# Three deformable convolutions and an expert network on one core: border rows skipped, side work paced by the tap

## The chip, the cores and the metric

The kernel runs on one core of a Trainium2 chip. The core has five engines, each with its own queue of instructions: TensorE (PE) multiplies matrices and transposes tiles, VectorE (DVE) does arithmetic on tiles in on-chip memory, ScalarE (ACT) copies, scales and evaluates functions, GpSimd (POOL) here issues the gathers, and SyncE (SP) issues most of the other transfers. Each engine works through its own instructions in order, so an instruction that waits holds up all that stand behind it on that engine. PE reads on-chip memory (SBUF) and writes accumulators (PSUM), from which ACT or DVE copies.

The metric is the time of one execution in microseconds (us). Three runs of the kernel before took 7496.17 to 7528.83 us, with a median of 7508.25 us.

## What is computed

The input is four images of 256 channels and 64 x 64 positions. Each image is normalised over its channels and goes through three layers of a modulated deformable 3 x 3 convolution. The result is added to the input, each position (token) is normalised, and a network of eight experts, of which the two likeliest are taken for each token, is added:

```python
om = conv3x3(x, w_off) + b_off            # zero padding; 27 channels
off, mask = om[:, :18], sigmoid(om[:, 18:])
ys, xs = grid + tap + off                 # for each of 9 taps
sampled = bilinear(x, ys, xs) * mask      # zero outside the image
x = relu(einsum('bikhw,oik->bohw', sampled, wk) + b)      # three times
t = tokens(image + x)
p, e = top_k(softmax(norm(t) @ gate_w + gate_b), 2)
out = t + sum(p * (gelu(norm(t) @ W1[e] + b1[e]) @ W2[e] + b2[e]))
```

The convolution in the first line is the offset convolution. Its input is padded with zeros, so at the first row of an image the upper row of taps adds nothing, and at the last row the lower one.

## The kernel before

**Blocks and stages.** An image is cut into eight blocks (n = 0 to 7) of eight rows, 512 positions each. One layer of one image is a stage. The twelve stages run in a fixed order, written as (layer, image): (0,0), (1,0), (0,1), (2,0), (1,1), (0,2), (2,1), (1,2), (0,3), (2,2), (1,3), (2,3). They are counted from 0 here. Except between stages 0 and 1, between 10 and 11, and at the end, a stage uses nothing that the stage just before it makes, and the pipeline runs on over its border.

**The main work of a block** is `main_block` (L482). For each of nine taps it takes four samples of 128 positions, in two pairs. For each sample (`samples`, L494), POOL gathers the four corners from a table in device memory (L503, ten buffers g), DVE combines them in two instructions (L509, L514, eight buffers s), and ACT scales the result (L517). Two pairs later (`LAG` = 2), `turn` (L521) lets PE transpose the pair into PSUM (L532, tag tp, three buffers) and ACT copy it to sT (L535). After the second pair, `finish` (L541) multiplies sT by the weights of the tap into the accumulator acc (L555). After the ninth tap ACT applies relu (L577). In layers 0 and 1 the result goes into a window, a tile of ten rows: the block's eight and one neighbouring row on each side.

**Windows and plans.** `window` (L281) takes a window's tile. In block 0 it sets the row above the image to zero with a memset on DVE (L290), in block 7 the row below (L292). `rows_done` (L295) copies the shared rows between neighbouring windows on ACT (L300, L301) and starts, for a finished block n, its `store_table` and the `off_block` of block n - 1 (in block 7 of both 6 and 7). `store_table` (L313) transposes the rows (L325), copies them (L328, tile hv, two buffers) and stores them into the table of the next layer, four transfers a time on SP. `off_block` (L345) makes the plan of a block for the next layer: 18 matmuls of the offset convolution into po (L357), a copy with bias on ACT (L366, tile om), four matmuls that turn it to positions (L371, tile pm, one of the three buffers with tag tp), tanh and a copy on ACT (L387 and L391, tiles th and pos), and then 14 short DVE instructions (L395 to L427) that give the row indices idx and the weights cf. The tiles om, th, pos and those of the 14 instructions have one buffer each.

**Other side work.** `pre_block` (L429) loads a block of an image, transposes it (L442), copies it (ACT L447), normalises it on DVE (L55 to L80, in which L62 takes the statistics and L78 writes the result h), stores it into the first table, transposes it back (L462) and fills a window. The first image is done ahead of all stages; image 1 beside stage 0, image 2 beside stage 3, image 3 beside stage 6. `tokens` (L587) follows each block of layer 2: it loads the image's rows (L596), adds them on DVE (L599), transposes (PE L608, ACT L613), multiplies by the gate (L618), stores t (L626), normalises (L62 to L78), stores z (L636), works out the softmax with an exponential on ACT (L661) and the sum on DVE (L665), and picks two experts. When a group of blocks is complete, its expert work is put into queues of small pieces (`routes`, `tiles`, `sums`), of which `pump` takes some after each tap of the later stages.

**What sets the order.** Each piece of side work is a Python generator whose `yield`s cut it into steps. `aside(steps, gen, plan)` (L997) puts it `steps` times into one of two lists, `plans_side` for `off_block` and `side` for the rest. After each tap k, `step` (L1001) takes from the front of each list the number of entries left, divided by the taps left (9 - k) and rounded up, and runs one step for each. One piece with seven entries alone in its list thus runs one step a tap; with two pieces in a list, two steps are run a tap, and both may belong to the same piece. `after(self.last)` places a DVE instruction of side work behind the newest L514. `settle` (L1012) empties both lists at the two dependent borders and at the end, with `draining` set while expert pieces are used up there; `starting` is set until the first stage begins. A scheduler then fixes each engine's final order from these issues and their dependences.

Of the kernel before, what the change touches and what calls it, by code (L numbers as in the profile page):

```python
# [117 lines left out]
class Weave:  # L118
# [162 lines left out]
    def window(self, n, nm, spare):  # L281

        if spare:
            if n % 2 == 0:
                self.spare = self.wt.tile([P, 2, WINN], F32, tag="wt", name=f"win_{nm}")
            w = self.spare[:, n % 2, :].rearrange("p (c r w) -> p c r w", c=CC, w=W)
        else:
            w = self.win.tile([P, CC, RPB + 2, W], F32, tag="win", name=f"win_{nm}")
        if n == 0:
            self.nc.vector.memset(w[:, :, 0, :], 0.0)  # L290
        if n == NB - 1:
            self.nc.vector.memset(w[:, :, RPB + 1, :], 0.0)  # L292
        return w

    def rows_done(self, l, b, n, wins):  # L295

        nc = self.nc
        w = wins[n]
        if n > 0:
            nc.scalar.copy(w[:, :, 0, :], wins[n - 1][:, :, RPB, :])  # L300
            nc.scalar.copy(wins[n - 1][:, :, RPB + 1, :], w[:, :, 1, :])  # L301
        if l > 0:
            self.aside(3, self.store_table(l, b, n, w))
        ready = [n - 1] * (n > 0) + [n] * (n == NB - 1)
        for m in ready:
            gen = self.off_block(l, b, m, wins[m])
            if self.starting and m >= NB // 2:

                self.later.append(gen)
            else:  # L310
                self.aside(6, gen, True)

    def store_table(self, l, b, n, w):  # L313

# [30 lines left out]
    def off_block(self, l, b, n, w):  # L345
# [4 lines left out]

        po = self.ps1.tile([P, BLK], F32, tag="po", name=f"po_{nm}")

        terms = [(ky, kx, c) for kx in (1, 0, 2) for ky in range(3) for c in range(CC)]
        for m, (ky, kx, c) in enumerate(terms):
            g = m % NQ
            x0, x1 = max(0, 1 - kx), min(W, W + 1 - kx)
            nc.tensor.matmul(  # L357
                po[g * Q : (g + 1) * Q, :].rearrange("q (r w) -> q r w", w=W)[:, :, x0:x1],
                lhsT=self.wo[l][:, 3 * ky + kx, c, :],
                rhs=w[:, c, ky : ky + RPB, x0 + kx - 1 : x1 + kx - 1],  # L360
                start=(m < NQ),
                stop=(m + NQ >= len(terms)),
                tile_position=(0, g * Q),
            )
# [26 lines left out]
        nc.scalar.copy(pos.rearrange("p (t k) d -> p t (k d)", k=K), pm[:, :, : 2 * K])  # L391
        yield
        yield
        with self.after(self.last):
            nc.vector.tensor_tensor(  # L395
                pos, pos, self.base[:, n].rearrange("p t k d -> p (t k) d"), ALU.add
# [32 lines left out]
    def pre_block(self, b, n, wins, spare):  # L429
# [8 lines left out]
        for t0 in range(0, TPB, 2):  # L438
# [7 lines left out]
                    )  # L446
            nc.scalar.copy(h[:, t0 : t0 + 2, :], tp)  # L447
        yield
        rest = normalise(nc, self.small, h, h, EPS_C, nm)
        with self.after(self.last):  # L450
            next(rest)
# [89 lines left out]
    def finish(self):  # L541
# [36 lines left out]
        if l < NL - 1:  # L578
            self.rows_done(l + 1, b, n, wins)
        else:  # L580
            self.aside(7, self.tokens(b, n, r))

# [2 lines left out]
    def tokens(self, b, n, r):  # L587
# [37 lines left out]
        nc.scalar.copy(lg, lp)  # L625
        nc.sync.dma_start(self.t_dram[b][n], tok)  # L626
        yield
        rest = normalise(nc, self.small, tok, z, EPS_T, nm)
        with self.after(self.last):
            mean = next(rest)  # L630
# [29 lines left out]
        )  # L660
        nc.scalar.activation(lg, lg, AF.Exp)  # L661
        yield
        sm = small("sm", (P, TPB))
        with self.after(self.last):
            nc.vector.tensor_reduce(sm, lg, AX.X, ALU.add)  # L665
# [335 lines left out]
    def step(self, k):  # L1001

        for side in (self.plans_side, self.side):
            for _ in range(-(-len(side) // (K - k))):
                next(side.pop(0), None)

    def after(self, newest):

# [26 lines left out]
    def run(self):  # L1035
# [36 lines left out]
        for i, (l, b) in enumerate(self.stages):  # L1072
            wins, pre = {}, {}
            for n in range(NB):
                for gen in self.later[:2]:
                    self.aside(6, gen, True)
                self.later = self.later[2:]
                self.main_block(i, n, wins)
                if i in beside:
                    self.aside(5, self.pre_block(beside[i], n, pre, i == 0))  # L1080
            if i + 1 == len(self.stages) or self.stages[i + 1] == (l + 1, b):
                while self.pairs:
                    self.turn()
# [52 lines left out]
```

## Time and profile before

| | before |
|---|---|
| median of three runs | 7508.25 us (7496.17 to 7528.83) |
| the profiled execution's own time | 7520.62 us |
| its span in the profile | 7518.9 us |
| mean clock granted to TensorE | 0.944 |
| PE busy | 6443.2 us, 86% |
| DVE busy | 4952.9 us, 66% |
| POOL busy | 4476.5 us, 60% |
| ACT busy | 3266.0 us, 43% |
| bytes read and written | 313 GB/s over the span |

The groups of the profile give a line's engine, its tile, count, busy time and mean ns, and behind the bar the idle time of the engine ahead of it and what ended that. These are the groups of the lines that the change touches or that wait near it:

```
L357 PE MATMUL po<-win,wo 128*32 128x504 f32 (+1 forms) x2304 | 366.0, 615 | 6.5 <-ACT win L301 4.2 <-ACT win L577 2.0
L357 PE MATMUL po<-win_pre,wo 128*32 128x504 f32 (+1 forms) x1152 | 184.2, 617 | 2.0 <-ACT om L366 2.0
L395 DVE TENSOR_TENSOR pos<-pos,base 128x72 f32<-128x72 f32 x96 | 22.0, 229 | 92.2 <-ACT pos L391 91.7 <-issue 0.5
L665 DVE TENSOR_REDUCE sm_tok<-lg_tok 128x4 f32<-128x32 f32 x32 | 5.8, 182 | 87.2 <-ACT lg_tok L661 83.2 <-ACT sT L535 4.0
L290 DVE MEMSET win<- 128x128 f32 x8 | 1.3, 165 | 72.9 <-PE po L357 71.6 <-PE tp L532 1.3
L292 DVE MEMSET win<- 128x128 f32 x8 | 1.3, 165 | 0.0
L290 DVE MEMSET win_pre<- 128x128 f32 x4 | 0.7, 165 | 26.2 <-PE po L357 25.3 <-PEq L1126 0.9
L292 DVE MEMSET win_pre<- 128x128 f32 x4 | 0.7, 165 | 10.0 <-PE po L357 10.0
```

po's 18 matmuls go to four column tiles of 32 in turn; the hardware lists each as two records, so 96 blocks give 3456. A tile's name carries the kind of block that made it: win_pre, h_pre and st_pre belong to `pre_block`, t_tok, st_tok, lg_tok and sm_tok to `tokens`. In the timeline, each row gives the start, the length, the engine, the line, the operation and, in brackets, the idle time before it with what ended it. "issue" is a wait for nothing that the profile shows, "remote" and "an unknown queue" one for something that it can't name, such as a transfer.

### The profile page before, as it was taken

To read this page: it belongs to the slowest core of one execution; us is meant where nothing else is said; L and a number is where in the kernel's file an instruction comes from. 1 tells how busy PE (TensorE), PEld (TensorE's weight loads), DVE (VectorE), ACT (ScalarE), POOL (GpSimd) and SP (SyncE) were. 2 spreads that over 40 slices of the span, in tenths; PEclk is the share of its full clock that TensorE was granted. 3 is DMA by queue.
4 is the path that set the end of the run, shared out by engine and by line. 5 is a ranking of instruction groups with operands and counts; after the bars stand their busy time and mean duration, and the time that the engine had idled before them with its cause. 6 is when DMAs were issued, how large, how long until landed. Compare 5 with 4: busy or idle time off the path is not lost.

```text
span 7518.9 us, 88985 instructions
## 1 busy us (share of the span) xinstructions
PE 6443.2 (86%) x26500; PEld 3618.8 (48%) x26500; DVE 4952.9 (66%) x11467; ACT 3266.0 (43%) x7141; POOL 4476.5 (60%) x4245
## 2 busy tenths in 40 slices
PE   6898888888898888889988888888888788977887
PEld 3443333334454444445554445444544555644565
DVE  6776777768887666567777556666768554667421
ACT  3444544445544444445443434444444333444322
POOL 4654666656666565556557656555656565666543
PEclk8999999999999999999999999999999899989998
DMA  8997999989998888888888888888888777888644
GB/s 266 337 325 274 352 342 335 346 331 356 362 349 311 300 305 297 278 315 322 314 293 316 293 280 314 295 302 294 308 306 299 251 271 240 288 302 287 211 139 123
DMA packets 800320, 2223.73 MB, mean 296 GB/s; under 512 B 104729, under 2 KB 302873, under 8 KB 794081
## 3 DMA queue, kind: packets, MB, share of 16 engines
q0 software_dynamic: 551200, 1947.35, 73.3%
q1 hardware_dynamic: 248640, 270.69, 10.9%
q8 instruction: 215, 3.52, 0.2%
q14 instruction: 265, 2.16, 0.1%
HBM read 2160.68 MB, written 196.40 MB: 313 GB/s over the span
## 4 chain that ended last, share of the span: by engine, by line
PE 69%; ACT 10%; issue 7%; another core or an unknown queue 6%; DVE 4%; DMA 2%; POOL 1%; SPq 0%; ACTq 0%; DVEq 0%; POOLq 0%
PE acc L555 34%; PE tp L532 10%; PE ph L856 7%; PE py L874 6%; PE po L357 6%; ACT sT L535 4%; ACT s L517 3%; DVE g L509 2%; DVE s L514 1%; PE pm L371 1%; ACT hT L866 1%; PE ftp L840 1%; ACT win L577 1%; PE tpv L325 1%
## 5 line engine op out<-in xcount | busy, mean ns | idle before, releaser
L503 POOL DMA_INDIRECT g<-tab,idx x3456 | 3685.4, 1066 | 2371.6 <-DVE s L514 1061.8
L555 PE MATMUL acc<-sT,wk 128*128 128x512 f32 x6912 | 3492.1, 620 | 253.4 <-ACT sT L535 147.5
L509 DVE SCALAR_TENSOR_TENSOR g<-g,cf 128x512 f32<-128x512 f32 x3456 | 2559.2, 742 | 269.1 <-DMA g<-tab,idx 245.5
L514 DVE SCALAR_TENSOR_TENSOR s<-g,cf 128x256 f32<-128x256 f32 x3456 | 1662.7, 483 | 1331.3 <-PE tp L532 729.9
L535 ACT COPY sT<-tp 128x512 f32<-128x512 f32 x1728 | 1002.0, 585 | 2312.0 <-PE tp L532 1553.0
L517 ACT ACTIVATE s<-s,cf 128x256 f32<-128x256 f32 x3456 | 1629.5, 508 | 256.7 <-DVE s L514 160.7
L555 PEld LDWEIGHTS acc<-sT,wk 128*128 128x128 f32 x6912 | 1198.9, 198 | 1106.7 <-issue 816.7
L532 PEld LDWEIGHTS tp<-ident,s 128*128 128x128 f32 x6912 | 893.2, 146 | 1666.2 <-issue 898.9
L532 PE MATMUL tp<-ident,s 128*128 128x128 f32 x6912 | 1287.3, 286 | 439.2 <-ACT s L517 253.8
L856 PE MATMUL ph<-fzT,w 128*128 128x256 f32 x2608 | 720.8, 411 | 78.0 <-ACT fzT L844 28.1
L874 PE MATMUL py<-w,hT 128*128 128x256 f32 x2608 | 671.1, 396 | 103.5 <-ACT hT L866 58.0
L856 PEld LDWEIGHTS ph<-fzT,w 128*128 128x128 f32 x2608 | 506.3, 205 | 212.9 <-issue 69.6
L874 PEld LDWEIGHTS py<-w,hT 128*128 128x128 f32 x2608 | 484.5, 196 | 242.0 <-issue 91.9
L866 ACT ACTIVATE hT<-ph,w 128x256 f32<-128x256 f32 x652 | 281.9, 471 | 616.3 <-PE ph L856 378.2
L812 POOL DMA_INDIRECT zt<-z,tok x326 | 333.8, 1024 | 161.5 <-issue 88.0
L800 POOL DMA_INDIRECT w<-in_W,wrow x163 | 178.0, 1092 | 381.2 <-issue 138.8
L357 PE MATMUL po<-win,wo 128*32 128x504 f32 (+1 forms) x2304 | 366.0, 615 | 6.5 <-ACT win L301 4.2
L892 DVE TENSOR_TENSOR y<-py,w 128x512 f32<-128x512 f32 x163 | 111.9, 686 | 341.5 <-PE py L874 285.1
L915 POOL DMA_INDIRECT gy<-ys,slots x256 | 255.6, 998 | 104.5 <-issue 70.0
L930 DVE SCALAR_TENSOR_TENSOR ta<-gy,cw,ta 128x256 f32<-128x256 f32 x256 | 120.6, 480 | 125.6 <-DMA gy<-ys,slots 78.4
L357 PE MATMUL po<-win_pre,wo 128*32 128x504 f32 (+1 forms) x1152 | 184.2, 617 | 2.0 <-ACT om L366 2.0
L366 ACT ACTIVATE om<-po,bo 128x512 f32<-128x512 f32 x96 | 65.9, 687 | 265.3 <-PE po L357 156.3
(154 smaller groups left out, 2961.0 us busy)
## 6 DMA issues: line engine op xcount, KB each, us to landing
tab<-hv SPq DMA_DIRECT2D x512, 128.0 KB
g<-tab,idx POOLq DMA_INDIRECT x3456
ys<-y SPq DMA_DIRECT2D x163, 256.0 KB
tab<-h_pre SPq DMA_DIRECT2D x128, 256.0 KB
wk<-in_conv_w SPq DMA_DIRECT2D x99, 256.0 KB
xc_pre<-in_x SPq DMA_DIRECT2D x32, 512.0 KB
xr_tok<-in_x SPq DMA_DIRECT2D x32, 512.0 KB
t<-t_tok SPq DMA_DIRECT2D x32, 512.0 KB
```

What stands on the lines that cost most here:

```text
L357: nc.tensor.matmul(po[g * Q : (g + 1) * Q, :].rearrange("q (r w) -> q r w", w=W)[:, :, x0:x1], lhsT=self.wo[l][:, 3 * ky + kx, c, :], rhs= ...
L503: self.gathered = nc.gpsimd.indirect_dma_start(out=g.rearrange("p x s f -> p (x s f)"), out_offset=None, in_=self.table(*self.stages[i]), ...
L509: nc.vector.scalar_tensor_tensor(g[:, :, 0, :], g[:, :, 1, :], cf[:, j, 0:1], g[:, :, 0, :], ALU.mult, ALU.add,)
L514: self.last = nc.vector.scalar_tensor_tensor(s, g[:, 1, 0, :], cf[:, j, 1:2], g[:, 0, 0, :], ALU.mult, ALU.add)
L517: nc.scalar.activation(s, s, AF.Copy, scale=cf[:, j, 2:3])
L532: self.turned = nc.tensor.transpose(tp[:, c, u * P : (u + 1) * P], ss[u][:, c * P : (c + 1) * P], self.ident)
L535: nc.scalar.copy(self.sT[:, :, t0 * P : (t0 + 2) * P], tp)
L555: nc.tensor.matmul(acc[:, o, :], lhsT=self.wk[k][:, c, o * P : (o + 1) * P], rhs=sT[:, c, :], start=(k == 0 and c == 0), stop=(k == K - 1 ...
L812: self.nc.gpsimd.indirect_dma_start(out=zt, out_offset=None, in_=grp.zd, in_offset=bass.IndirectOffsetOnAxis(ap=grp.tok[:, j : j + 1], axi ...
L856: nc.tensor.matmul(ph[:, h, :], lhsT=w1[:, o : o + P], rhs=zT[:, c, :], start=(c == 0), stop=(c == CC - 1),)
L866: nc.scalar.activation(ht[:, h, :], ph[:, h, :], AF.Gelu, bias=w1[:, k : k + 1])
L874: nc.tensor.matmul(py[:, u, :], lhsT=hT[h // 2][:, h % 2, u * P : (u + 1) * P], rhs=w2[:, h * C : (h + 1) * C], start=(h == 0), stop=(h == ...
```

## The change

Three things change.

1. `window` no longer zeroes a row. The offset convolution of block 0 leaves the upper image row out of the matmuls with ky = 0, and that of block 7 the lower row of those with ky = 2: six of the 18 matmuls then have seven rows in place of eight, 448 or 441 columns for 512 or 504. In block 0 the order of ky becomes 1, 2, 0, so that the first matmul into each column tile writes all rows.
2. `step` runs at most one step of each generator a tap: it passes over the entries of generators that it has already moved in this tap, and falls back to the front of the list where there is no other.
3. `pause` gives one more `yield`, except while `starting` or `draining`, at four places ahead of a DVE part: in `off_block` before L395, in `pre_block` before the normalisation, in `tokens` before the normalisation and before the sum L665. The counts of steps grow with it: `off_block` from 6 to 7, `tokens` from 7 to 9, `pre_block` from 5 to 6.

```diff
--- before.py
+++ after.py
@@ -286,10 +286,6 @@
             w = self.spare[:, n % 2, :].rearrange("p (c r w) -> p c r w", c=CC, w=W)
         else:
             w = self.win.tile([P, CC, RPB + 2, W], F32, tag="win", name=f"win_{nm}")
-        if n == 0:
-            self.nc.vector.memset(w[:, :, 0, :], 0.0)
-        if n == NB - 1:
-            self.nc.vector.memset(w[:, :, RPB + 1, :], 0.0)
         return w
 
     def rows_done(self, l, b, n, wins):
@@ -308,7 +304,7 @@
 
                 self.later.append(gen)
             else:
-                self.aside(6, gen, True)
+                self.aside(7, gen, True)
 
     def store_table(self, l, b, n, w):
 
@@ -350,14 +346,17 @@
 
         po = self.ps1.tile([P, BLK], F32, tag="po", name=f"po_{nm}")
 
-        terms = [(ky, kx, c) for kx in (1, 0, 2) for ky in range(3) for c in range(CC)]
+        top, low = int(n == 0), int(n == NB - 1)
+        kys = (1, 2, 0) if top else (0, 1, 2)
+        terms = [(ky, kx, c) for kx in (1, 0, 2) for ky in kys for c in range(CC)]
         for m, (ky, kx, c) in enumerate(terms):
             g = m % NQ
             x0, x1 = max(0, 1 - kx), min(W, W + 1 - kx)
+            y0, y1 = top * (ky == 0), RPB - low * (ky == 2)
             nc.tensor.matmul(
-                po[g * Q : (g + 1) * Q, :].rearrange("q (r w) -> q r w", w=W)[:, :, x0:x1],
+                po[g * Q : (g + 1) * Q, :].rearrange("q (r w) -> q r w", w=W)[:, y0:y1, x0:x1],
                 lhsT=self.wo[l][:, 3 * ky + kx, c, :],
-                rhs=w[:, c, ky : ky + RPB, x0 + kx - 1 : x1 + kx - 1],
+                rhs=w[:, c, ky + y0 : ky + y1, x0 + kx - 1 : x1 + kx - 1],
                 start=(m < NQ),
                 stop=(m + NQ >= len(terms)),
                 tile_position=(0, g * Q),
@@ -391,6 +390,8 @@
         nc.scalar.copy(pos.rearrange("p (t k) d -> p t (k d)", k=K), pm[:, :, : 2 * K])
         yield
         yield
+        for _ in self.pause():
+            yield
         with self.after(self.last):
             nc.vector.tensor_tensor(
                 pos, pos, self.base[:, n].rearrange("p t k d -> p (t k) d"), ALU.add
@@ -446,6 +447,8 @@
                     )
             nc.scalar.copy(h[:, t0 : t0 + 2, :], tp)
         yield
+        for _ in self.pause():
+            yield
         rest = normalise(nc, self.small, h, h, EPS_C, nm)
         with self.after(self.last):
             next(rest)
@@ -578,7 +581,7 @@
         if l < NL - 1:
             self.rows_done(l + 1, b, n, wins)
         else:
-            self.aside(7, self.tokens(b, n, r))
+            self.aside(9, self.tokens(b, n, r))
 
 
 
@@ -625,6 +628,8 @@
         nc.scalar.copy(lg, lp)
         nc.sync.dma_start(self.t_dram[b][n], tok)
         yield
+        for _ in self.pause():
+            yield
         rest = normalise(nc, self.small, tok, z, EPS_T, nm)
         with self.after(self.last):
             mean = next(rest)
@@ -660,6 +665,8 @@
         )
         nc.scalar.activation(lg, lg, AF.Exp)
         yield
+        for _ in self.pause():
+            yield
         sm = small("sm", (P, TPB))
         with self.after(self.last):
             nc.vector.tensor_reduce(sm, lg, AX.X, ALU.add)
@@ -1001,8 +1008,15 @@
     def step(self, k):
 
         for side in (self.plans_side, self.side):
+            moved = []
             for _ in range(-(-len(side) // (K - k))):
-                next(side.pop(0), None)
+                i = next((i for i, gen in enumerate(side) if gen not in moved), 0)
+                moved.append(side.pop(i))
+                next(moved[-1], None)
+
+    def pause(self):
+
+        return range(0 if self.starting or self.draining else 1)
 
     def after(self, newest):
 
@@ -1073,11 +1087,11 @@
             wins, pre = {}, {}
             for n in range(NB):
                 for gen in self.later[:2]:
-                    self.aside(6, gen, True)
+                    self.aside(7, gen, True)
                 self.later = self.later[2:]
                 self.main_block(i, n, wins)
                 if i in beside:
-                    self.aside(5, self.pre_block(beside[i], n, pre, i == 0))
+                    self.aside(6, self.pre_block(beside[i], n, pre, i == 0))
             if i + 1 == len(self.stages) or self.stages[i + 1] == (l + 1, b):
                 while self.pairs:
                     self.turn()
```

## The prediction

> **What bounds the kernel now.** The order of reading is: busy times, chain, VectorE's waits, the timeline at the longest of them, then windows over whole blocks, which give the price.
>
> First the page's busy times and the engine shares of the chain that ended last:
>
> ```profile
> PE 6443.2 (86%) x26500; PEld 3618.8 (48%) x26500; DVE 4952.9 (66%) x11467; ACT 3266.0 (43%) x7141; POOL 4476.5 (60%) x4245
> ...
> PE 69%; ACT 10%; issue 7%; another core or an unknown queue 6%; DVE 4%; DMA 2%; POOL 1%; SPq 0%; ACTq 0%; DVEq 0%; POOLq 0%
> ```
>
> TensorE (PE) is the bound, with 7518.9 - 6443.2 = 1076 us idle. An edit can win only part of that idle time, matmul columns, or a lower clock. Next, what VectorE (DVE) waits for, with sum, count and longest in us:
>
> ```profile
> DVE s L514 <- PE tp L532: 729.9, 626, 9.2
> DVE pos L395 <- ACT pos L391: 91.7, 21, 11.0
> DVE sm_tok L665 <- ACT lg_tok L661: 83.2, 13, 9.0
> DVE win L290 <- PE po L357: 71.6, 6, 14.7
> DVE st_pre L62 <- ACT h_pre L447: 52.6, 12, 9.1
> DVE win_pre L290 <- PE po L357: 25.3, 2, 14.7
> ```
>
> The first is the healthy one: DVE has filled all eight s buffers and waits for PE to free one. The others stop DVE behind a side instruction; rows 2, 3 and 5 are what the pauses delay, rows 4 and 6 are the memsets. The timeline at one memset, a row each of DVE, POOL, ACT and PE (start, length; in brackets the idle time before and what ended it):
>
> ```profile
> 1085.53 0.17 DVE L290 MEMSET win<- 128x128 f32 x1 [10.59 <-PE po L357]
> ...
> 1087.05 1.21 POOL L503 DMA_INDIRECT g<-tab,idx  x1 [10.89 <-DVE s L514]
> ...
> 1104.17 0.58 ACT L328 COPY hv<-tpv 128x512 f32<-128x512 f32 x1 [6.45 <-remote]
> ...
> 1105.22 0.69 PE L532 MATMUL tp<-ident,s 128*128 128x128 f32 x2 [6.32 <-ACT s L517]
> ```
>
> The memset needs a free window, freed only when PE has read an old one. DVE stops 10.6 us, POOL cannot gather 10.9 us, then gathers come in a burst. The hv copy waits 6.5 us for its buffer, ScalarE (ACT) stands, and PE starves 6.3 us. Windows over a quiet block and over this one, the last of its stage (us, PE, PEld, DVE, ACT, POOL busy, PE clock, DMA share, GB/s), then the recovery alone:
>
> ```profile
> 995.80:1051.80 56.00, 50.06 (x197) 22.78 (x197) 43.47 (x87) 28.39 (x64) 38.60 (x36) 1.00 0.95 354
> 1051.80:1118.30 66.50, 53.67 (x202) 24.26 (x203) 45.19 (x91) 29.27 (x65) 37.33 (x36) 0.95 0.86 323
> ...
> 1097.00:1105.00 8.00, 1.33 (x4) 0.30 (x2) 5.67 (x13) 1.42 (x3) 4.73 (x6) 0.78 1.04 408
> ```
>
> The block is 10.5 us longer, at clock 0.95, and in the recovery PE works 1.3 of 8 us. Stages 3 and 9 have no such stall, and their last blocks are still about 4 us over their neighbours (all nine wk loads are there). So one bad memset costs about 7 us, 0.66 per us of stall. It varies: stages 4 and 7 have stalls of 12.2 and 14.7 us, yet last blocks no longer than expected. PE idle in excess of its usual 0.105 per us, counted from a stall's start to 25 us behind it, gives over the memsets of row 0 27.4 us in eight events, largest 7.1.
>
> **The change part by part.**
>
> *Memsets.* 24 instructions of 0.165 us go (4 us of DVE, hidden: DVE is 34% idle), and with them 109 us of wait (72.9 + 26.2 + 10.0 in the groups of L290 and L292). Block lengths give four stalls at 7 us (stages 1, 2, 5, 8), one at 5 (stage 6), 2 for the rest: 35 us. The lower end is 15 (half of the excess idle of 27.4: a delay that PE makes good later), the upper 60 (109 us at the rate 7/10.6 = 0.66, less what stages 4 and 7 show). I take 35, the block count, because it contains the clock. Late next is the border plan, below.
>
> *Columns.* 24 border blocks shorten 6 of 18 po matmuls each by 1/8, 288 records. The four column tiles overlap: 28 records in one run took 3.52 us, 0.126 each, while the row's mean of 615 ns counts each in full. That gives 288 x 0.126 / 8 = 4.5 us; in full it would be 288 x 0.615 / 8 = 22. I take 5, as the run is the wall time. At n = 0 the middle ky now comes first, with equal count; runs of po matmuls are 272 for 278 in the built order. Zero.
>
> *Off-block pause.* From the pos copy on ACT to the add on DVE the built order has four taps of 5.9 us for three. Usual blocks wait nothing either way. In four blocks of image 1's preparation, 1.5 taps become 1.75, which ends waits of about 4 us each beside stage 0, at no loss of PE: zero. The plan has up to five taps left until it is used.
>
> *One step a tap per piece.* This moves most at the stage borders, where the plans of blocks 6 (A) and 7 (B) are both made in the next stage's block 0. Before, A ran all its steps, then B; B's add stood two taps behind its pos copy. Now they alternate; but A's tiles th and pos have one buffer, so B's tanh and pos copy stand in ACT's order behind A's last reads, and B's add on DVE follows 0.25 tap later. DVE runs almost two taps ahead of PE and ACT, so it will wait. How long can be read where before had slack: at one such border the last two rows below are DVE's sample and ACT's scale of two samples later in the same tap.
>
> ```profile
> 1183.15 0.48 DVE L514 SCALAR_TENSOR_TENSOR s<-g,cf 128x256 f32<-128x256 f32 x1
> ...
> 1191.27 0.91 ACT L517 ACTIVATE s<-s,cf 128x256 f32<-128x256 f32 x2
> ```
>
> DVE is done at 1183.63, ACT at 1192.18: 8.5 us. The ten such places give 11.2, 7.1, 8.5, 7.0, 1.0, 4.4, 7.3, 8.2, 14.6 and 7.3, together 76.6 us. Queued behind this add on DVE are the next samples, behind these POOL's gathers and ACT's scales: the memset's pattern. Its price there: the seven memset stalls at stage ends, 86.8 us, cost 33, or 0.38 per us; so 29. The lower end is 0: seven border waits of pos before (43 us, such as 6.0 at 1156.55) leave PE no excess idle, and they go. The upper is ten times 7.1 = 71. I take 29, since the memset is the nearest stall in length. In eight places B's 18 po matmuls also stand as one lump behind A's, before a transpose, where part was spread: 8 x 0.8 = 6 us (0 to 16, two gaps of 0.98 us, the time of a short run). pm then holds one of three tp buffers some five taps. The copy that frees a tp buffer ends 0.6 us after its transposes, so two serve the pairs: zero.
>
> The Trainium skill, "Perfetto Trace Analysis", section "Optimization Strategy", speaks against this: the same gap repeated on the engine that should be full can mean too few buffers for the next tile. By it the 0.68 us gap of a tap would come once more in 8 x 5 taps, 27 us, and the sum would be -22 instead of -49. The trace of before, with pm held briefly, shows neither.
>
> *Token pauses.* The fourteen waits of L665 for the exponential (87.2 us) have 27.0 us of excess PE idle behind them. In stages 9 and 11 the distance grows from 1 tap to 2, in stage 3 from 0.75 to 1.25, in stage 6 it stays 1.0. Waits of 50.7 + 4.0 of 87.2 us therefore go: 27.0 x 0.63 = 17 (10 to 27). The add of xr moves a tap nearer its load: it had 14 to 18 us, has 7 to 10, and landings take 3.5 to 9.5. In a bad case DVE waits 3 us; inside the lower end.
>
> *Statistics pauses.* ACT L447 to the statistics grows from 0.75 to 2.75 taps, ACT L613 from 1.5 to 3: thirteen waits with 8.8 us of excess, of which 7 go. PE's own wait for the normalised h (L462 on L78, up to 4.75 us at 1885.26) mostly goes, as PE's transposes now stand half a tap from it for 1.5: about 25 us of stages 3 and 6, of which I take 20, PE having other waits soon after. Together 27 (5 to 34). SP's stores of t, z and tab and POOL's piece queue move by a tap; the tables are read two stages later and the experts run beside later stages, so zero. Were that cover gone, one tap of 5.9 us per group.
>
> *Sum.* Gains 35 + 5 + 17 + 27 = 84, losses 29 + 6 = 35: -49. The profiled execution took 7520.62, so 7471.6; it lies 12.4 us above the median of the runs, 7508.25, against which it is **7459**.
>
> **The rivals.**
> - *More than the sum* (0.15). "issue" and "unknown queue" hold 13% of the chain, 1019 us; bursts of gathers feed them. Six per cent fewer, 61 us, gives about 7398. For: DMA share 1.04 in the recovery. Against: these shares also stand in stages without a memset.
> - *Nothing to measure* (0.25). DVE's lead absorbs most stalls, as in stages 4 and 7, and stage 6's sums don't move: 7471 to 7545. For: 27 us of excess idle for 109 us of wait. Against: the 10.5 us block.
> - *Slower* (0.19). The border wait takes the memset's place, ten times 7.1 plus lumps of 16 = 87, against gains at their low ends, 15 + 5 + 10 + 5 = 35: +52, 7560. With central gains it turns the sign beyond 7.8 us a place, with low gains beyond 3. For: it holds DVE and POOL at the same place of the pipeline. Against: the old border waits cost nothing.
>
> **How the numbers follow.** A measurement of this kernel tells about 0.5%, 37.5 us: faster is below 7470.7, slower above 7545.8. The forecast, 7425 to 7470, has 0.41; with the first rival, faster is 0.56, same 0.25, slower 0.19. The range goes from 7385 (upper gains in part) to 7565.
>
> **What the profile after would show.** No rows L290 and L292; hv's wait for "remote" (32.4) near nothing; pos waiting about 80 to 100 us for ACT in some ten waits of 7 to 15 us at the first blocks of stages; st and sm waits under half; last blocks of stages 1 and 2 near 60 us and first blocks longer. I am wrong if the last blocks stay at 67, if the border waits starve PE by more than 7 us each, or if tp buffers show up before L532.

## The result, and the profile after

The changed kernel is slower: 7569.73 us (median of six runs, 7564.73 to 7584.75) against 7503.91 us for six runs of the kernel before (7487.89 to 7528.83), a ratio of 1.009 with a 95% interval of 1.0072 to 1.0107. Forecast were 7459 us and a gain. The profiled execution has a span of 7563.0 us, 44 us longer than that of before.

One fact is needed before anything else is read. All experiments ran in a second setting, where the kernel before takes about 6805 us instead of 7504. The record names five chips for them, which agree (medians of 6803 to 6808 us); which chip gave the first setting is not on record, nor what its condition was. In the second setting the same changed kernel is not slower (0.9988). So each ratio below is against the kernel before in the same setting, and the text says which.

The page after, first setting, busy times and chain:

```profile
PE 6419.9 (85%) x26500; PEld 3590.7 (47%) x26500; DVE 4959.8 (66%) x11443; ACT 3269.2 (43%) x7141; POOL 4447.2 (59%) x4245
...
PE 69%; ACT 10%; issue 8%; another core or an unknown queue 6%; DVE 3%; DMA 2%; POOL 1%; SPq 0%; ACTq 0%; DVEq 0%; POOLq 0%
```

TensorE is busy 23 us less and idle 67 us more. VectorE's waits after, first setting (sum, count, longest):

```profile
DVE pos L396 <- ACT pos L390: 121.3, 27, 13.0
DVE r L602 <- DMA xr_tok<-in_x: 81.1, 13, 9.6
DVE r L602 <- ACT r L580: 46.8, 8, 10.3
DVE st_pre L62 <- ACT h_pre L448: 26.7, 6, 10.5
DVE sm_tok L672 <- ACT lg_tok L666: 20.0, 10, 4.3
DVE z_tok L78 <- DMA tab<-h_pre: 19.6, 6, 5.6
```

The memsets' waits are gone; those of the sum fell from 83 to 20 us and of the image statistics from 53 to 27. But pos rose from 92 to 121, and two waits are new: the addition of xr (L602) waits 128 us for the load and for the relu, and z's write (L78) for stores of the image's table.

Where the time went in us, by stage (from the first transpose, L532 before and L535 after, of each stage to that of the next; stage 11 with all behind it). "Second" is the same pair in the second setting, from e5 and e6 below:

| stage | 0 | 1 | 2 | 3 | 4 | 5 | 6 | 7 | 8 | 9 | 10 | 11 |
|---|---|---|---|---|---|---|---|---|---|---|---|---|
| first, before | 570.6 | 474.6 | 477.2 | 493.1 | 552.8 | 589.5 | 594.7 | 635.7 | 590.9 | 574.8 | 756.1 | 1109.5 |
| after less before | -8 | -11 | -9 | +22 | +10 | -27 | -3 | +12 | -6 | +15 | +73 | -23 |
| second, before | 524.1 | 449.0 | 449.6 | 460.1 | 501.7 | 519.4 | 528.3 | 538.0 | 524.0 | 514.7 | 689.1 | 1009.5 |
| after less before | -8 | -1 | +1 | +23 | +1 | -2 | +7 | +14 | -1 | +4 | -33 | -2 |

In the first setting the last blocks of stages 1 to 9 are together 60 us shorter, the first two blocks of these stages 43 us longer, and stage 10, for which the forecast had no term but a zero, 73 us longer. Stage 3 loses 22 to 23 us in both settings. Stage 10 has opposite signs.

The answer to the memset block shown before, now in the first setting after and then in the second setting before and after (windows over the last block of stage 1; us, PE, PEld, DVE, ACT, POOL busy, PE clock, DMA share, GB/s):

```profile
1065.70:1123.70 58.00, 50.10 (x198) 22.83 (x197) 43.30 (x86) 28.42 (x63) 38.11 (x36) 1.00 0.99 372
```

```profile
1015.90:1071.90 56.00, 50.06 (x198) 22.80 (x197) 41.89 (x84) 28.55 (x63) 32.10 (x31) 1.00 0.85 325
```

```profile
1006.30:1062.30 56.00, 50.06 (x198) 22.79 (x197) 43.61 (x87) 28.44 (x63) 37.98 (x36) 1.00 0.98 373
```

Measured by the same transposes, this block took 68.1 us at clock 0.92 in the first setting before, and takes 58.0 after. In the second setting it takes 56.0 with the memset and 56.0 without. And the stall is there, to a hundredth, in the second setting's timeline of the kernel before:

```profile
1024.96 0.17 DVE L290 MEMSET win<- 128x128 f32 x1 [10.60 <-PE po L357]
```

VectorE stood 10.60 us (10.59 in the first setting), and TensorE had no gap of 2 us in this block. The stall that the forecast priced at 7 us costs nothing there.

What was different in the first setting shows in the trace of before, in its records of semaphores, the counters by which engines signal each other. The forecast read the hv copy at 1104.17 as waiting for its buffer, that is for an old store. But in the trace ScalarE's waits for the four transfers of that store end at 1097.25, and the last landing recorded for them is at 1051.83. The copy began 0.02 us after a signal of TensorE at 1104.15, and the transposes that it copies have their modelled end at 1095.85. So TensorE's 6.3 us without work followed from a TensorE result that was told 8.3 us late. In the second setting the copy at the same place (1035.36) waits for nothing. Whether the memset's burst of gathers made that result late is not shown.

### The profile page after: what moved, and what is told of

It reads as the page before. It is cut to its first block, busy times and chain, and to the rows that moved or that the text cites. A ratio compares the mean times of both kernels' runs of the same rounds, so it can differ in the third digit from the quotient of the medians.

```text
span 7563.0 us, 88984 instructions
## 1 busy us (share of the span) xinstructions
PE 6419.9 (85%) x26500; PEld 3590.7 (47%) x26500; DVE 4959.8 (66%) x11443; ACT 3269.2 (43%) x7141; POOL 4447.2 (59%) x4245
## 4 chain that ended last, share of the span: by engine, by line
PE 69%; ACT 10%; issue 8%; another core or an unknown queue 6%; DVE 3%; DMA 2%; POOL 1%; SPq 0%; ACTq 0%; DVEq 0%; POOLq 0%
PE acc L558 34%; PE tp L535 11%; PE py L881 7%; PE ph L863 6%; PE po L356 6%; ACT sT L538 4%; ACT s L520 3%; PE pm L370 1%; DVE g L512 1%; PE ftp L847 1%; DVE s L517 1%; ACT hT L873 1%; PE tpv L321 1%; PE lp_tok L621 1%
## 5 line engine op out<-in xcount | busy, mean ns | idle before, releaser
L535 PEld LDWEIGHTS tp<-ident,s 128*128 128x128 f32 x6912 | 887.7, 145 | 1854.9 <-issue 1003.0
L535 PE MATMUL tp<-ident,s 128*128 128x128 f32 x6912 | 1308.4, 285 | 519.9 <-ACT s L520 294.0
L558 PEld LDWEIGHTS acc<-sT,wk 128*128 128x128 f32 x6912 | 1181.5, 197 | 1064.1 <-issue 778.0
L881 PE MATMUL py<-w,hT 128*128 128x256 f32 x2608 | 686.3, 403 | 97.3 <-ACT hT L873 50.7
L863 PEld LDWEIGHTS ph<-fzT,w 128*128 128x128 f32 x2608 | 490.0, 200 | 214.3 <-issue 79.6
L356 PE MATMUL po<-win,wo 128*32 128x504 f32 (+3 forms) x2304 | 358.8, 604 | 10.9 <-ACT win L580 8.0
L922 POOL DMA_INDIRECT gy<-ys,slots x256 | 261.6, 1022 | 96.7 <-issue 71.9
L356 PE MATMUL po<-win_pre,wo 128*32 128x504 f32 (+3 forms) x1152 | 185.5, 598 | 1.2 <-ACT om L365 1.2
```

Of the source, the lines that this page charges most:

```text
L356: nc.tensor.matmul(po[g * Q : (g + 1) * Q, :].rearrange("q (r w) -> q r w", w=W)[:, y0:y1, x0:x1], lhsT=self.wo[l][:, 3 * ky + kx, c, :], ...
L535: self.turned = nc.tensor.transpose(tp[:, c, u * P : (u + 1) * P], ss[u][:, c * P : (c + 1) * P], self.ident)
L558: nc.tensor.matmul(acc[:, o, :], lhsT=self.wk[k][:, c, o * P : (o + 1) * P], rhs=sT[:, c, :], start=(k == 0 and c == 0), stop=(k == K - 1 ...
L863: nc.tensor.matmul(ph[:, h, :], lhsT=w1[:, o : o + P], rhs=zT[:, c, :], start=(c == 0), stop=(c == CC - 1),)
L881: nc.tensor.matmul(py[:, u, :], lhsT=hT[h // 2][:, h % 2, u * P : (u + 1) * P], rhs=w2[:, h * C : (h + 1) * C], start=(h == 0), stop=(h == ...
```

## The experiments

Theories at the start: the plans' alternation at the stage borders holds VectorE ("border"); the tokens' pauses let the experts of image 2 begin a tap later, and that hurts stage 10 ("late group"); the one-step rule brings the addition of xr too near its load ("late sum"). All ratios are to the kernel before, run beside it.

**e1 to e4: parts of the change.** e1 keeps only the first part (a cut of its edit):

```diff
-        if n == 0:
-            self.nc.vector.memset(w[:, :, 0, :], 0.0)
-        if n == NB - 1:
-            self.nc.vector.memset(w[:, :, RPB + 1, :], 0.0)
...
+            y0, y1 = top * (ky == 0), RPB - low * (ky == 2)
```

> Only the skipped border rows and the memsets' removal are kept; the side steps run as before. Theory 'memset' (the memsets cost what the last blocks of the stages showed, 61 us over the twelve stages in the two profiles): about 7444. Theory 'cover' (the gain of the memsets' removal comes back at the next wait, whatever the steps do): 7490 to 7510. The changed kernel's stage 10 (756.1 us before, 828.6 after) should stay near 756 in both.

e2 adds the new `step`, without any pause:

```diff
+                i = next((i for i, gen in enumerate(side) if gen not in moved), 0)
+                moved.append(side.pop(i))
```

> The skipped rows and the one-step-a-tap rule, without any of the four pauses. Theory 'border' (plans A and B of the stage border alternate and hold VectorE; the first two blocks of all stages were 44 us longer in the changed kernel): 7444 + 44 = about 7488, with pos waiting at ten borders. Theory 'late group' (the loss lies in stage 10, because the tokens' two pauses let the expert work of image 2 begin a tap later): stage 10 near 756 and the whole near 7444 to 7488. If the rule itself puts the expert work in stage 10 into a bad place, stage 10 is near 828 here already.

e3 has e1's part and the four pauses with the old `step`:

```diff
+        for _ in self.pause():
+            yield
```

> The skipped rows and the four pauses, with the old rule for the steps. Theory 'border': the first blocks as before, 7444 or, with the pauses' gain in stage 0, 7424. Theory 'late group': stage 10 longer by about 70, so 7510. Theory 'late sum' (the addition of xr stands nearer to its load because of the one-step rule, 128 us of new VectorE waits): no such waits here.

e4 is the changed kernel with

```diff
-        put(3, lambda: self.begin(grp))
+        put(2 if grp.b == 2 else 3, lambda: self.begin(grp))
```

> The changed kernel, but the expert work of image 2 begins one tap earlier (2 taps behind its last inversion in place of 3), which undoes the tap that the pauses of the tokens add there. Theory 'late group': stage 10 falls from 828 to about 760 and the whole to 7500 to 7520. Theories 'border' and 'late sum': 7570, stage 10 unchanged.

Measured: e1 1.0007 (0.9998 to 1.0016), e2 1.0035 (1.0023 to 1.0048), e3 0.9928 (0.9915 to 0.9940), e4 1.0044 (1.0032 to 1.0057). The rows and memsets are worth nothing here. The rule without the pauses costs 14 us (e2 less e1), the pauses without the rule win some 50 (e3 less e1), and e4 fell the wrong way: it was meant to repair the changed kernel. Stage 10 took 692.7, 690.5, 656.2 and 691.2 us; only e3 has the experts on the later tap. So the later tap is a gain in this setting, and "late group" falls here.

**e5 to e8: both kernels, and the rule for one list at a time.** e5 and e6 are the kernel before and the changed one, unaltered. e7 and e8 restrict the rule:

```diff
                 i = next((i for i, gen in enumerate(side) if gen not in moved), 0)
+                i = i if side is self.plans_side else 0     # e7
+                i = i if side is self.side else 0           # e8
```

> The kernel before, unchanged, for a trace beside the other runs of this call. If this chip is like that of the first experiments, where the kernel before took 6804.7 us: stage 10 near 690, stage 3 near 460, and no result of TensorE that arrives later than its modelled end. If it is like that of the first measurement, 7500.

> The changed kernel, unchanged. Theory 'rule' (the one-step-a-tap rule costs what the first experiments showed in stages 3 and 10, the pauses gain about 45): on a chip like the first experiments' 6795 to 6835, which is a ratio of 0.999 to 1.004. Theory 'late results' (the loss of the first measurement was that chip's late TensorE results, 122 places with 485 us for 110 with 416): a ratio at or below 1.000 where there are none, 1.009 where there are.

> The changed kernel with the one-step-a-tap rule for the list of the plans alone; the other list is stepped from its front as before. Theory 'border' (plans A and B alternate at the stage borders and hold VectorE): as slow as the changed kernel. Theory 'late sum' (the rule brings the addition of xr to within a tap of its load): 20 to 30 us faster than the changed kernel, with stage 3 back near 460 and xr waits of 10 us in total.

> The changed kernel with the one-step-a-tap rule for the other list alone (tokens, image preparation, tables); the plans are stepped from the front as before. Theory 'border': as fast as rows and pauses without the rule, 0.993 of the kernel before. Theory 'late sum': as slow as the changed kernel, xr waits of 40 to 80 us in total.

Measured: e5 6807.83 us in its one run, e6 0.9988 (0.9978 to 0.9999), e7 0.9935 (0.9921 to 0.9948), e8 0.9985 (0.9976 to 0.9994). e7 is as fast as e3 without the rule (6760.88 and 6759.84 us), though its pos waits show the alternation (71.9 us, longest 10.7, against 27.5 and 4.4 in e3). "Border" falls in this setting. The other list's rule is the whole cost, 6797.04 - 6760.88 = 36 us, and e8, which has it alone, is as slow as e6.

Where e6 loses it is stage 3 first of all, 483.2 us against 462.8 in e7. VectorE's waits in the last five blocks of that stage, in e6 and in e7:

```profile
DVE z_tok L78 <- DMA tab<-h_pre: 14.9, 4, 4.3
```

```profile
DVE s L517 <- PE tp L535: 5.3, 5, 1.1
DVE st_tok L62 <- ACT t_tok L616: 4.5, 5, 1.3
```

and one block of e6 there:

```profile
1812.00:1873.00 61.00, 54.20 (x230) 26.72 (x229) 55.19 (x152) 31.91 (x69) 37.60 (x36) 1.00 0.96 362
```

z shares two buffers (tag b) with the images' h and the tokens' t. Under the old rule the tokens and the image's preparation take turns of several steps; under the new one they advance together, and z's write comes while h is still being stored to the table. It waits 3.0 to 4.3 us a block, on an engine that is busy 55.19 of 61 us there. This is not a cheap engine in stage 3.

**e9 and e10: the two causes alone.** e9 is the changed kernel with

```diff
-        z = self.big.tile([P, TPB, C], F32, tag="b", name=f"z_{nm}")
+        z = self.big.tile([P, TPB, C], F32, tag="z", bufs=1, name=f"z_{nm}")
```

> The changed kernel, but the normalised tokens z have a buffer of their own instead of sharing the two buffers of tag b with the images' h and the tokens' t. In stages 3 and 6 of the changed kernel z's write (L78) waits 3.0 to 4.3 us a block for the table stores of h to land, in a stage where VectorE is busy 92% of the time. Theory 'buffer' (the one-step rule costs by bringing z's write to within a tap or two of h's stores): stage 3 falls from 483 to about 463 and stage 6 by a few us, the whole from 6797 to about 6770 on a chip like the last two calls'. Theory 'late sum' (the xr load is what is late): no change in stage 3.

and e10 the kernel before with

```diff
-        put(3, lambda: self.begin(grp))
+        put(4 if grp.b == 2 else 3, lambda: self.begin(grp))
```

> The kernel before, but the expert work of image 2 begins one tap later (4 taps behind its last inversion in place of 3), as the pauses of the tokens make it do in the changed kernel. Theory 'phase' (that tap decides whether the fetch of an expert's weights and the combining gathers of image 1 fall into the same tap, and is all that the pauses win in stage 10): stage 10 falls from 689 to about 656 and the whole from 6805 to about 6770, ratio 0.995. If the first measurement's loss in stage 10 (756 to 828) came from the same tap, then on such a chip this kernel is about 1.01 of the kernel before. Theory 'pauses themselves': no change, 1.000.

Measured: e9 0.9964 (0.9949 to 0.9978), 6776.36 us, 21 less than e6 (16 by the two ratios, whose intervals just meet at 0.9978); no wait of z is left, and stages 3 and 7 fall from 483.2 to 473.1 and from 552.1 to 543.4. "Late sum" can be the rest, but no run tests it: the xr waits stayed (46.7 us for the load, 36.6 in e6), and stage 3 kept 10 of its 20 us. e10 0.9943 (0.9931 to 0.9956): one number, a tap of delay, wins 34 us. Why is in VectorE's waits of stage 10, in e5 and in e10:

```profile
DVE g L509 <- DMA g<-tab,idx: 177.1, 80, 10.6
```

```profile
DVE g L509 <- DMA g<-tab,idx: 121.7, 129, 5.5
```

and in e5's timeline there:

```profile
5383.86 0.75 DVE L509 SCALAR_TENSOR_TENSOR g<-g,cf 128x512 f32<-128x512 f32 x1 [6.10 <-DMA g<-tab,idx]
...
5403.31 0.75 DVE L509 SCALAR_TENSOR_TENSOR g<-g,cf 128x512 f32<-128x512 f32 x1 [6.04 <-DMA g<-tab,idx]
...
5423.01 0.75 DVE L509 SCALAR_TENSOR_TENSOR g<-g,cf 128x512 f32<-128x512 f32 x1 [6.29 <-DMA g<-tab,idx]
```

A sample's gather is 6 us late every 20 us, which is every second tap (a tap of this stage takes 9.6 us). On POOL's queue in e5 the fetch of an expert's weights (w) and the gathers that combine image 1 (gy) stand in the same tap, every second one:

```profile
5392.37 1.15 POOL L800 DMA_INDIRECT w<-in_W,wrow  x1 [3.13 <-ACT s L517]
...
5396.51 0.97 POOL L915 DMA_INDIRECT gy<-ys,slots  x1 [0.30 <-issue]
...
5411.64 1.15 POOL L800 DMA_INDIRECT w<-in_W,wrow  x1 [2.89 <-ACT s L517]
...
5415.78 1.14 POOL L915 DMA_INDIRECT gy<-ys,slots  x1 [0.30 <-issue]
```

In e10 they alternate, with four gathers of samples between them:

```profile
5415.25 1.01 POOL L800 DMA_INDIRECT w<-in_W,wrow  x1 [0.31 <-issue]
...
5424.09 0.96 POOL L915 DMA_INDIRECT gy<-ys,slots  x1 [0.30 <-issue]
...
5436.53 1.00 POOL L800 DMA_INDIRECT w<-in_W,wrow  x1 [3.02 <-ACT s L517]
...
5445.79 1.02 POOL L915 DMA_INDIRECT gy<-ys,slots  x1 [0.30 <-issue]
```

Most of the lateness is then gone: in stage 10, VectorE waits over 3 us for a sample's gather 22 times in e5 and 7 times in e10.

**e11 and e12: the pauses, with and without that tap.** Only the pauses (e3's edit without e1's), and in e12 `put(2 if grp.b == 2 else 3, ...)` besides.

> The four pauses alone: memsets and full rows as in the kernel before, old rule for the steps. Theory 'phase': the pauses win the tap of image 2's experts (34 us in the last call) and some 10 us in stage 0: about 6760, ratio 0.993 to 0.994, as with the rows skipped (6759.8); the rows and memsets are then worth nothing here. If the memsets cost something once the other waits are gone: 6770 or more.

> The four pauses alone, and the expert work of image 2 one tap earlier (2 for 3), which takes back the tap that the tokens' pauses add. Theory 'phase': the 34 us go, about 6795, ratio 0.998 to 0.999, stage 10 near 690. Theory 'waits' (the pauses win by the VectorE waits that they end, as the forecast said, 44 us): 6760, as without the shift.

Measured: e11 0.9939 (0.9925 to 0.9952), e12 0.9985 (0.9976 to 0.9994), both as the theory "phase" said. The waits that the pauses end are worth 6805.7 - 6798.54 = 7 us; the other 36 are the tap.

So the second setting adds up: rows and memsets 0, pauses -7, their side effect on the experts' tap -36, the rule for the plans 0, the rule for the other list +36, together -7; measured 6797.04 - 6804.8 = -8. These come from four groups of runs, whose medians of the kernel before lie between 6803.3 and 6805.7 us. The 36 of the rule is itself read from e6, so this agreement is in part built in; what it tests is that e7, with rows, pauses and the rule for the plans, takes e11's time (6760.88 and 6762.62 us). The terms also depend on each other: the rule costs 14 us without the pauses and 36 with them.

**e13 to e18: what is different in the first setting.** Its traces hold waits that the profile puts down to "remote", and the second setting's hold none. In stage 10, first setting, before and after:

```profile
ACT sT L535 <- remote: 63.2, 13, 12.0
ACT hT L866 <- remote: 36.3, 7, 9.1
...
DVE s L514 <- remote: 15.2, 6, 6.8
```

```profile
DVE s L517 <- remote: 102.2, 26, 14.7
ACT hT L873 <- remote: 74.6, 15, 8.3
...
ACT sT L538 <- remote: 39.6, 20, 6.6
```

One of them in the timeline after, first setting:

```profile
5953.96 0.60 PE L535 MATMUL tp<-ident,s 128*128 128x128 f32 x4
...
5959.80 0.58 ACT L538 COPY sT<-tp 128x512 f32<-128x512 f32 x1 [1.30 <-remote]
5959.80 0.48 DVE L517 SCALAR_TENSOR_TENSOR s<-g,cf 128x256 f32<-128x256 f32 x1 [5.71 <-remote]
...
5960.85 0.69 PE L535 MATMUL tp<-ident,s 128*128 128x128 f32 x2 [6.28 <-ACT sT L538]
```

The copy reads what these transposes write, and VectorE needs the s buffer that they free. Both start at the same instant, 5.2 us after the transposes' modelled end. So the result of TensorE was told late. The records of semaphores bear this out: all 295 "remote" waits before, and 299 of 300 after, ended on the one semaphore that TensorE alone counts up, 95% of them within 0.1 us of the recorded signal. Of the 228 signals that end them before, 79 came at half clock, the others at full. These records are incomplete in the first setting (4249 of TensorE's signals before, 5156 in e5), so its sums for "remote" and "issue" are rough. Half a clock would make 0.60 us into 1.20, not 5.84. In the whole execution VectorE's s waits 220.2 us for "remote" before and 279.0 after. The theory "late results": such lateness takes VectorE's lead, so that the same waits now cost. To try it in the second setting, kernels repeat a pair's transposes at 157 of 864 taps; the values stay the same:

```diff
-        for u in range(2):
+        late = t0 == 0 and ((i * NB + n) * K + k) % 11 in (3, 7)
+        for u in [0, 1] * (9 if late else 1):          # 19 in e17 and e18
```

The 9 holds for e13 to e16. e13 is the kernel before, e14 the changed one, e15 has e1's part, e16 e10's tap.

> The kernel before; at 157 of its 864 taps TensorE repeats the four transposes of a pair eight times more (32 more transposes, about 4 us at 0.13 us each), so that its results come late there, spread over all taps of a block. It is the reference of the next three. At most 157 x 4.2 = 660 us longer than the kernel before.

> The changed kernel with the same late taps. Theory 'late results' (late TensorE results take VectorE's lead, so that each VectorE wait of the changed kernel reaches TensorE): slower than the kernel before with the same late taps by 0.5% or more. Theory 'something else on the first chip': the ratio of the two stays at 0.999, as without late taps.

> Rows skipped and memsets gone, nothing else, with the same late taps. Theory 'late results': the memset stalls now cost, so this is faster than the kernel before with late taps by 0.3% or more (up to 60 us). Otherwise equal, as 1.0007 without late taps.

> Only the experts of image 2 a tap later, with the same late taps. If late results turn the sign of that tap: slower than the kernel before with late taps, stage 10 longer. Otherwise 30 to 40 us faster, as without.

Measured, against the kernel before without lateness: e13 1.0221 (1.0207 to 1.0236), e14 1.0165 (1.0151 to 1.0179), e15 1.0227 (1.0213 to 1.0241), e16 1.0210 (1.0196 to 1.0223). The changed kernel is the faster by 35 us, the rows stay worth nothing, and the tap loses its gain. A row of e13 shows 38 transposes in 4.31 us, 0.113 each, so some 570 us of them were added (157 x 32 x 0.113), of which only 145 reached the end. So the last two add 72 transposes a tap in place of 32. e17 is the kernel before, e18 the changed one.

> The kernel before; the four transposes of a pair are repeated eighteen times at 157 taps (72 more, about 8 to 9 us), so that the time lost comes nearer to the 700 us by which the first chip is slower: 7300 to 7700.

> The changed kernel with the same lateness. Theory 'late results': slower than e17 by 0.3% or more. Theory 'something else on the first chip': equal or faster, as with half the lateness (6916 against 6951).

Measured: e17 7830.82 us, 1.1504 (1.1488 to 1.1520), e18 7769.39 us, 1.1409 (1.1390 to 1.1428). The changed kernel is 0.8% faster, at a time beyond the first setting's. Lateness of TensorE spread over the taps does not turn the sign. "Late results" in this form falls. The form is not quite the first setting's: these taps give TensorE work (it is idle 377 us in e13), where the late results of the first setting leave it idle (1076 us before).

The fastest measured is e3, rows and pauses with the old rule (0.9928), with e7 beside it. Both beat both kernels in the second setting. Neither ran in the first.

## Why the prediction was wrong

The measured loss is the first setting's, and most of it, in stage 10, has no cause yet. Three steps are shown to be wrong by the runs of the second setting: zero for the experts' tap (-36 us), no price for the one-step rule in the list of the other pieces (+36 us), and 7 us for a memset stall (0, and read from a wait that had another cause). The signs that the forecast set itself came mostly true, which did not help: the last blocks of stages 1 and 2 took 58.0 and 56.6 us, hv's wait for "remote" fell from 32.4 to 7.9, the sum's from 83 to 20. None of them looked at stages 3 and 10.

- **"Memsets ... I take 35".** In the first setting the blocks that it was read from are 60 us shorter after, but the first two blocks of the same stages are 43 longer, and rows and memsets were not run alone there, so what the memsets were worth in it stays open. In the second setting the step is wrong: 0 (e1, and e11 against e3). The stall is the same 10.6 us; what differs is whether TensorE runs dry behind it. The forecast explained that by a store that holds hv's buffer. The row said only "remote", and the trace shows that the wait was for a late TensorE result, while the store had long landed. The upper end of this term, 60, is also too high by its own working: 109 us less the 26.9 of stages 4 and 7, at 0.66, give 54.
- **"Border" 29 + 6.** Where it stands was right (pos waits of 71.9 to 121.3 us, longest 10.7 to 13.0, where 80 to 100 in waits of 7 to 15 were foretold). The price in the second setting is the lower end, 0 (e7 against e3, e8 against e6, each within 2 us). In the first setting the two first blocks of stages 1 to 9 grew by 43 us, but they grew by 21 in the second too, where the border costs nothing, so this can't be given to it.
- **"Token pauses" 17 and "statistics pauses" 27.** Of 44 us, 7 were measured (e12). The waits went as foretold; they had mostly been covered.
- **"POOL's piece queue move by a tap; ... so zero".** This is the step that failed most in the second setting: that tap is worth -36 us, where all that the forecast priced as a gain brought 7, because it sets which transfers fall together. The forecast asked only whether the work was still in time. Its price for lost cover, "one tap of 5.9 us per group", was the wrong kind of price.
- **"One step a tap per piece" was priced for the plans' list alone.** The cost was in the other list: +36 us (e6 against e7), of which 16 to 21 come from a buffer shared by z and h (e9) and the rest is open. The forecast counted the xr load and put it inside a lower end; it did not ask whose buffer the moved write needs. It also took VectorE's idle share, 34%, from the whole kernel, though the windows of the profile before show it busy 421.86 of 493.10 us in stage 3.
- **"Off-block pause", zero.** Perhaps too low: stage 0 is 8 us shorter after in both settings, and 515.0 us in e12 for 524.1 in e5, where the pos waits of this stage fell from 26.7 to 15.6. In the first setting these waits did not fall (32.1 before, 33.8 after), and the statistics pause stands in stage 0 too, so the 8 us can't be given to one of them.
- **"Columns" 5.** po's two groups are busy 544.3 us after and 550.2 before, 6 less (counting overlaps in full); in time it can't be seen.
- **The tp buffers.** Zero was taken where pm holds one of the three for five taps. e7, which keeps that, is not slower than e3, so this held in the second setting. The forecast also gave an estimate of 27 us by the rule of the Trainium skill, "Perfetto Trace Analysis", section "Optimization Strategy", that a gap repeated on the engine that should be full can mean too few buffers; no run shows them.

The rival "slower", 7560 us, came near the number, but its mechanism, the border wait at ten places, costs nothing in the second setting and is shown by no run of the first; as far as the runs tell, it came near by luck. **What stays open** is the first setting's loss of 66 us. Of the 44 us between its two profiles, stage 3's 22 are the same size in both settings. In the second the rule for the other list makes them, about half by the shared buffer (e9). In the first no run parts them, though the same waits stand there (19.6 us of z, 81.1 of xr for its load). Stage 10's 73 are not explained. The windows over stage 10, before and after in the first setting (columns as above):

```profile
5653.30:6409.40 756.10, 649.75 (x2753) 407.68 (x2753) 437.35 (x981) 300.19 (x662) 447.48 (x428) 0.93 0.78 265
```

```profile
5647.60:6476.20 828.60, 673.55 (x2777) 412.07 (x2778) 441.17 (x983) 308.67 (x669) 438.64 (x429) 0.91 0.72 243
```

TensorE is idle 49 us more and, at the lower clock, busy 24 us more. VectorE's wait for gathers fell there as in e10 (145.3 to 76.8 us), so the tap did its work, but the rows for "remote" above, which are late TensorE results, rose. e13 to e18 show that spread lateness alone does not turn the sign. Why the results are late, and why more so in stage 10 after the change, no run tells.

## What to carry to other kernels

A stall's price belongs to the stage and to the chip's condition in which it was read; look first whether the bound engine runs dry behind it and which signal ended the wait that it runs dry on, and take the busy share of that stage, not of the kernel. When a piece of work moves by one step, ask two things besides whether it is still in time: which buffers its writes share with the work that it now stands beside, and which periodic transfers it now coincides with. A gain or loss below 1% should be seen in more than one setting before its cause is told.

## What was not expected of the hardware

- The same kernel takes 7504 us in one setting and 6805 in the other, with equal work (26500 matmuls in each trace): TensorE is idle 1076 and 584 us, and the clock record has 137 and 51 stretches at half speed, 849 and 307 us together.
- In the first setting TensorE results are told several us after their modelled ends (before, the sT copy alone waits 371.9 us for "remote"); the traces of the other have no such wait. The page "TensorE: Matmul & The Clock Gate" of the Trainium skill, section "Part 1: The HAM clock gate", says that low clock is the default and activity releases it. The rows agree as far as they go: in the window from 5959 to 5961 of the profile after the granted clock is 0.50, behind a stretch without any matmul. The late results are more than that clock explains: 0.60 us of transposes would take 1.20 at half clock, and took 5.84.
- 157 delays of about 3.6 us (32 transposes of 0.113 us) on the bound engine cost 145 us in all; with 72 transposes, about 8.1 us, they cost 1023.
